# Layer 1 of a four-layer convolution and scan network: other piece boundaries, another order of directions, the last image in chunks

## The chip, the cores and the metric

The kernel runs on one core of a Trainium2 chip. The core has TensorE (PE), VectorE (DVE), ScalarE (ACT), GpSimd (POOL) and SyncE (SP, which here only issues transfers). Each engine works through its own list of instructions in order; an instruction that waits for another engine holds up all that stand behind it. The metric is the time of one execution on the device in microseconds, the median of three runs.

## The reference, cut to what matters

Four layers follow one another on 8 images of 64 channels and 64 x 64 pixels. Only layer 1 is changed. Its reference is this (weights and reshapes left out):

```python
xn = ln(x, 1e-6);  xm, z = split(xn @ in_proj)
xm = silu(conv3x3_depthwise(xm) + conv_b)            # u, 128 channels
xs = [rows, columns, rows reversed, columns reversed]  # 4 directions of u
dts, B, C = split(xs @ x_proj);  delta = softplus(dts @ dt_w + dt_b)
h = exp(delta * A) * h + delta * B * u ;  y = sum_n h * C    # scan over 4096 pixels, 16 states n
y = sum over the 4 directions of y  +  u * sum(D)
y = ln(y, 1e-5) * silu(z);  x1 = x + y @ out_proj
h = conv3x3_depthwise(conv1x1(ln(x1, 1e-6)))
out = x1 + conv1x1(gelu(h1) * h2)
```

Three normalisations over channels (of x, of y, of x1), one depthwise convolution of u and one of the hidden layer belong to each image beside the four scans.

## The kernel before, in words

**The scan stream.** `stream` (L383) works through steps. A step is one image, one direction k and one chunk j of 1024 pixels, and has 16 slots, one for each state n. There are 8 x 4 x 4 = 128 steps and 2048 slots in layer 1. A slot i issues: on POOL the product `hb` = du*B for slot i+2 (L434); on DVE the scan of slot i (L450); the product of the scan with C (L464), on DVE for eleven of the sixteen states and on POOL for states 1, 4, 7, 10 and 13 ("shared"); on PE four matmul instructions that add the product of slot i-2 to the accumulator `acc` (`gather`, L276); on ACT the exponential `dA` of slot i+2 (L441) and the copy of the last column, `carry` (L1148). `dA` has 2 buffers, `hb` and `hc` have 3, `acc` has 1. At the end of a step `drain` (L1157) adds `acc` to the image's y: for direction k = 0 it is a copy on ACT (L1163), for the other three an addition on DVE (L1165); for the two column directions, k = 1 and 3, the view of y is strided.

**The work between the slots.** Everything else of an image is written as a generator that yields between pieces. `Task` (L217) wraps one; `advance` (L367) issues one piece of the first task in the queue `behind` in each slot. A piece that ends with `yield True` holds the only PSUM buffer for such work (`pp`, one buffer of 128 x 1024, tile `mm`); after `yield` it is free; after `yield False` the next piece does not need it. Three tasks belong to an image: `begin` (L905: normalisation, convolution, u and z), `finish` (L966: normalisation of y, product with z, projection, statistics of the next normalisation) and `feed` (L1015: the hidden layer). When the last step of image b is done, `done` (L1167) appends finish(b), begin(b+2) and feed(b), so that they run in the slots of image b+1.

**Pieces of the hidden layer.** `group` (L1041) issues a convolution as two halves (L842) and a right side (L850), one piece each; then the reader comes in the next piece: Gelu on ACT (L1054), a product on DVE (L1057), Gelu on ACT (L1065). The readers of the other convolution and of the projection are ACT's L951 and L1002.

**The next step's inputs.** `Step.prepare` (L1113) is a task as well: x_proj on PE, the copy `dbl` on ACT (L1120), dt_w on PE (L1128), softplus on ACT (L365), `du` on POOL (L1135). It begins at slot `start` = 1 of the step before. At that slot the loop first runs `while self.held or self.urgent: self.advance(behind)`: all pieces up to the one that gives the PSUM buffer back are issued at once. While prepare holds the buffer, no piece that needs it is issued.

**The end.** After the last slot, what is left in `behind` is issued without any slots: finish and feed of the last image.

Of the kernel before, what the change touches and what calls it, by code (L numbers as in the profile page):

```python
# [16 lines left out]
NB = 8  # L17
# [218 lines left out]
            self.step()  # L236


class Net:
    def __init__(self, ctx, tc, d):  # L240
        self.tc, self.nc, self.d = tc, tc.nc, d
# [138 lines left out]
                return  # L380
            queue.popleft()

    def stream(self, pools, ahead, steps, behind):  # L383

# [139 lines left out]
            decay(i + 2)  # L524
        steps[-1].drain(acc.pop(len(steps) - 1))
        steps[-1].done()
        while behind or self.urgent:
            self.advance(behind)

# [256 lines left out]
    def layer1(self, src, dst):  # L786
        nc, tc, d = self.nc, self.tc, self.d
        mid = self.hbm["x1a"]
        with ExitStack() as ctx:
# [2 lines left out]
            pp = pool("pp", 1, space=PSUM)  # L792
            bp = pool("b", 4), pool("cc", 5)
            pools = (bp, pool("hb", 3), pool("hc", 3), pool("h", 3), pool("pe", 2, space=PSUM), pool("pa", 1, space=PSUM))
            hp, h1 = pool("h3", 3, space=DRAM), pool("h1", 4, space=DRAM)
            hz = pool("hz", 1, space=DRAM).tile([NB, 128, L], F32, name="hz")
            centd, cent1 = self.load(cp, "centd"), self.load(cp, "cent1")
# [55 lines left out]

            def place(rows, normed, g, b):

                for r in range(2):
                    yield False
                    at = slice(r * C, r * C + C)
                    nc.scalar.activation(
                        rows[at, :, 1 + r : 1 + r + HW],  # L860
                        normed[at].rearrange("p (a b) -> p a b", b=HW),
                        AF.Identity,
                        bias=b[at],
                        scale=g[at],
                    )

            def statistics(hold, centred, halves, eps):

                rs = p1.tile([128, 32], F32, name="rs")
                for c in range(4):
                    ps = yield from centred(c)
                    sq = tp.tile([128, T], F32, name="tmp")
                    nc.scalar.activation(sq, ps, AF.Square)
                    yield
                    ps = pp.tile([128, T], F32, name="mm")
                    if halves:
                        for r in range(2):  # L880
                            at, o = slice(r * C, r * C + C), slice(r * 512, r * 512 + 512)
                            nc.tensor.matmul(ps[:1, o], mean[at, 0:1], sq[at, o], start=True, stop=True)
                    else:
                        self.mm(ps[:1], mean[:, 1:2], sq)
                    yield True
                    ms = tp.tile([1, T], F32, name="tmp")
                    nc.scalar.copy(ms, ps[:1])
                    nc.scalar.dma_start(rs[c * 32 : c * 32 + 32, :], ms.rearrange("o (p e) -> o p e", e=32))
                    yield
                yield False  # L890
                nc.scalar.activation(rs, rs, AF.Sqrt, bias=eps)
                yield False
                nc.vector.reciprocal(rs, rs)
                yield False
                hold["rs"] = h1.tile([1, L], F32, name="rs")
                nc.sync.dma_start(hold["rs"].rearrange("o (p e) -> (o p) e", e=32), rs)
                yield False
                yield False

# [5 lines left out]
            def begin(b):  # L905
# [37 lines left out]
                for c in range(4):  # L943
                    yield
                    ps = pp.tile([128, T], F32, name="mm")
                    for half in range(2):
                        conv_half(ps, taps, slice(0, 128), pad, c * 16, half)
                        yield True
                    conv_right(ps, taps, slice(0, 128), pad, c * 16)
                    yield True  # L950
                    nc.scalar.activation(hold["u"][:, c * T : c * T + T], ps, AF.Silu, bias=cb)  # L951
                for c in range(4):
                    yield
# [9 lines left out]
                    nc.scalar.activation(z, ps, AF.Silu)  # L963
                    nc.scalar.dma_start(hz[b, :, c * T : c * T + T], z)

            def finish(b):  # L966

                q, rows = b // 2, slice((b % 2) * C, (b % 2) * C + C)
                hold = images[b]
                y = hold.pop("y")  # L970

                def centred(c):
                    ps = pp.tile([128, T], F32, name="mm")
                    self.mm(ps, cent1, y[:, c * T : c * T + T])
                    yield True
                    return ps

                yield from statistics(hold, centred, False, self.eps5)

                def output(c):  # L980
                    at = slice(c * T, c * T + T)
                    inv = spread(hold, c)
                    z = tp.tile([128, T], F32, name="tmp")
                    nc.sync.dma_start(z, hz[b, :, at])
                    x = tokens(src, b, c)
                    yield False
                    yield
                    nc.gpsimd.tensor_tensor(inv, inv, z, ALU.mult)
                    ps = pp.tile([128, T], F32, name="mm")
                    self.mm(ps, cent1, y[:, at])  # L990
                    yield True
                    yield True
                    nc.vector.tensor_tensor(inv, ps, inv, ALU.mult)
                    yield
                    ps = pp.tile([128, T], F32, name="mm")
                    self.mm(ps, w_bias, z, start=True, stop=False)
                    yield True
                    self.mm(ps, w_out, inv, start=False, stop=False)
                    self.sides(ps, self.ident2, x, start=False)
                    yield True  # L1000
                    x = tp.tile([128, T], F32, name="tmp")
                    nc.scalar.copy(x, ps)  # L1002
                    nc.scalar.dma_start(mid[q, rows, at], x[:C])
                    yield
                    ps = pp.tile([128, T], F32, name="mm")
                    for r in range(2):
                        side, o = slice(r * C, r * C + C), slice(r * 512, r * 512 + 512)
                        nc.tensor.matmul(ps[:, o], centd[side], x[side, o], start=True, stop=True)
                    yield True
                    return ps  # L1010

                hold["again"] = {}
                yield from statistics(hold["again"], output, True, self.eps6)

            def feed(b):  # L1015

                q, rows = b // 2, slice((b % 2) * C, (b % 2) * C + C)
                ahead = {}
# [22 lines left out]
                def group(c, cols):  # L1041
                    ps = pp.tile([128, T], F32, name="mm")
                    o = ps[: cols.stop - cols.start]
                    for half in range(2):
                        conv_half(o, hidden, cols, strips[c % 2], 0, half)
                        yield True
                    conv_right(o, hidden, cols, strips[c % 2], 0)
                    yield True
                    return ps

                def gated(c):
# [8 lines left out]
                    ps = yield from group(c, slice(256, 362))  # L1060

                    h = tp.tile([106, T], F32, name="tmp")
                    if c < 2:
                        fetch(c + 2)
                    nc.scalar.activation(h, ps[:106], AF.Gelu)  # L1065
                    yield True
# [11 lines left out]
                    nc.scalar.dma_start(dst[q, rows, c * T : c * T + T], o)  # L1078
                    yield

                fetch(0)
                fetch(1)
                yield False
# [12 lines left out]

            behind = deque()
            begun = {}

            class Step:  # L1100
                start, early, late = 1, 8, True
                shared = (1, 4, 7, 10, 13)
                shaped = staticmethod(lambda t: t)

# [8 lines left out]
                def prepare(self):  # L1113
# [7 lines left out]
                    self.bc = hp.tile([NS, 2, T], F32, name="bc")  # L1121
                    for m in range(2):
                        nc.scalar.dma_start(self.bc[:, m, :], dbl[4 + m * NS : 4 + m * NS + NS])
                    yield
                    pt = pp.tile([128, T], F32, name="mm")
                    for r in range(2):
                        at, o = slice(r * C, r * C + 4), slice(r * 512, r * 512 + 512)
                        nc.tensor.matmul(pt[:, o], dtw[at, k, :], dbl[at, o], start=True, stop=True)  # L1128
                    yield True
                    yield True  # L1130
                    dt = self.dt = p2.tile([128, T], F32, name="dt")
                    net.softplus_act(dt, pt, dtb[:, k : k + 1])
                    yield False
# [22 lines left out]

                def drain(self, acc):  # L1157
                    hold = images[self.b]
                    if self.k == 0 and self.j == 0:
                        hold["y"] = img.tile([128, L], F32, name="img")  # L1160
                    y = view(hold["y"], self.k, self.c)
                    if self.k == 0:
                        nc.scalar.copy(y, like(acc, y))  # L1163
                    else:
                        nc.vector.tensor_tensor(y, like(acc, y), y, ALU.add)  # L1165

                def done(self):  # L1167
                    b = self.b
                    if self.k == 3 and self.j == 3:
# [7 lines left out]
            with tc.manual_schedule():  # L1177
                Task(begin(0)).run()
                if NB > 1:
                    begun[1] = Task(begin(1))  # L1180
                    behind.append(begun[1])
                steps = [Step(b, k, j) for b in range(NB) for k in range(4) for j in range(4)]
                self.stream(pools, (5, 2, 3), steps, behind)


    def layer2(self, src, dst):
# [742 lines left out]
```

## Time and profile before

| what | value |
|---|---|
| median of 3 runs (lowest, highest) | 25963.23 us (25957.64, 25969.22) |
| the profiled execution | 25946.79 us |
| its span | 25944.9 us |
| first scan of layer 1 | 1338.72 us from the span's start |
| last addition of the stream (L1165) | 8808.84 us |
| first matmul of layer 2 (L1229) | 9081.63 us |
| DVE busy in the whole span | 22293.5 us (86%) |
| POOL busy | 21525.5 us (83%) |
| PE busy | 21876.6 us (84%) |
| ACT busy | 14863.5 us (57%) |

The rows of the profile name an engine, a line of the kernel, an operation, its output and inputs by tile names, the busy time and the idle time of the engine just before, with what ended that idle time. A line can be a helper's: L276 is any full-width matmul. A table by windows gives the busy time of each engine in a stretch of the span. DVE and POOL durations overlap a little from one instruction to the next, so sums of durations lie slightly above the time taken.

### The profile page before, as it was taken

The numbers are of one execution on the slowest core, as the hardware profiler recorded it, in microseconds if no ns is written. First come the engines' busy times: TensorE is split into PE (matmuls) and PEld (weight loads), VectorE is DVE, ScalarE is ACT, GpSimd is POOL, SyncE is SP. The second block draws the span as 40 slices with busy tenths as digits, with TensorE's granted clock in tenths as the row PEclk, the third lists the DMA queues.
The fourth block names the chain that finished last, engine by engine and source line by source line (L and its number), as shares of the span: only waits on it lengthen the run. The fifth ranks groups of instructions, "written<-read, shape, count | busy, mean of one in ns | idle before, by whom it ended". The sixth has DMA issues, their size and how long they took to land. (4 is left out here: it accounts for less than half of the span.)

```text
span 25944.9 us, 197961 instructions
## 1 busy us (share of the span) xinstructions
PE 21876.6 (84%) x55754; PEld 8468.4 (33%) x55754; DVE 22293.5 (86%) x12878; ACT 14863.5 (57%) x18690; POOL 21525.5 (83%) x10141
## 2 busy tenths in 40 slices
PE   8777888888888778888888888888878888888888
PEld 5522333333333223322233333333333333333333
DVE  4389889889889579933799999999989999999999
ACT  4355555555555355522566666666666666666666
POOL 0089888889888559930799999999989999999999
PEclk9888999999999899988899999999999999999999
DMA  2289888888888558840455555555544555555554
GB/s 59 78 309 322 296 313 307 297 308 308 298 304 307 189 210 324 324 104 17 130 169 169 170 170 169 169 167 171 168 155 166 170 167 171 170 167 168 169 171 157
DMA packets 1775246, 5292.30 MB, mean 204 GB/s; under 512 B 536624, under 2 KB 542964, under 8 KB 1706304
## 3 DMA queue, kind: packets, MB, share of 16 engines
q1 hardware_dynamic: 1743936, 5207.12, 58.9%
q10 hardware_dynamic: 27136, 63.34, 0.8%
q0 software_dynamic: 3072, 9.18, 0.2%
q8 instruction: 443, 7.26, 0.1%
q14 instruction: 659, 5.40, 0.1%
HBM read 5122.15 MB, written 156.11 MB: 203 GB/s over the span
## 5 line engine op out<-in xcount | busy, mean ns | idle before, releaser
L434 POOL TENSOR_TENSOR hb<-du,bc 128x1024 f32<-128x1024 f32 x4608 | 10755.4, 2360 | 489.9 <-DVE h L450 330.7
L276 PE MATMUL acc<-hc,ident 128*128 128x512 f32 x18816 | 8903.1, 615 | 75.9 <-DVE img L1165 50.9
L441 ACT ACTIVATE dA<-dt,w_A 128x512 f32<-128x512 f32 x8192 | 5662.3, 691 | 4113.5 <-DVE hc L464 3125.0
L450 DVE TENSOR_TENSOR_SCAN dA<-dA,hb 128x1024 f32<-128x1024 f32 x3384 | 7724.8, 2283 | 226.6 <-POOL hb L434 132.9
L276 PE MATMUL acc<-h,ident 128*128 128x512 f32 x7808 | 4584.0, 717 | 2483.9 <-POOL h L464 2483.6
L434 POOL TENSOR_TENSOR hb<-du,b 128x1024 f32<-128x1024 f32 x2048 | 4834.6, 2387 | 736.3 <-DVE h L450 471.5
L276 PEld LDWEIGHTS acc<-hc,ident 128*128 128x128 f32 x18816 | 3685.6, 200 | 5278.5 <-issue 4614.8
L464 DVE TENSOR_TENSOR hc<-dA,bc 128x1024 f32<-128x1024 f32 x3296 | 4034.4, 1224 | 262.1 <-issue 11.1
L441 ACT ACTIVATE dA<-dt,w_l_A 128x1024 f32<-128x1024 f32 x2560 | 2856.1, 1117 | 1126.1 <-DVE hc L464 769.5
L450 DVE TENSOR_TENSOR_SCAN dA<-dA,carry,hb 128x1024 f32<-128x1024 f32 x1320 | 3093.9, 2344 | 205.2 <-ACT dA L441 92.9
L276 PEld LDWEIGHTS acc<-h,ident 128*128 128x128 f32 x7808 | 1557.2, 217 | 5163.9 <-POOL h L464 3334.2
L450 DVE TENSOR_TENSOR_SCAN h<-dA,hb 128x1024 f32<-128x1024 f32 x1352 | 3082.1, 2280 | 80.1 <-ACT carry L1148 43.0
L464 POOL TENSOR_TENSOR h<-h,bc 128x1024 f32<-128x1024 f32 x1312 | 3093.8, 2358 | 14.2 <-DVE h L450 14.2
L464 DVE TENSOR_TENSOR hc<-dA,c 128x1024 f32<-128x1024 f32 x1408 | 1723.4, 1224 | 116.8 <-DMA c<-bc 4.4
L464 POOL TENSOR_TENSOR h<-h,c 128x1024 f32<-128x1024 f32 x640 | 1515.5, 2368 | 30.4 <-ACT carry L1148 30.3
L450 DVE TENSOR_TENSOR_SCAN h<-dA,carry,hb 128x1024 f32<-128x1024 f32 x600 | 1403.5, 2339 | 112.6 <-ACT dA L441 74.0
L441 ACT ACT_TABLE_LOAD x1119 | 1435.7, 1283 | 23.6 <-DVE h L450 3.7
L1148 ACT COPY carry<-dA 128x1 f32<-128x1 f32 x1056 | 166.7, 158 | 1570.9 <-DVE hc L464 1512.3
L1796 PE MATMUL mm<-xn,taps 128*128 128x512 f32 x2048 | 937.8, 600 | 34.1 <-POOL xn L1762 31.9
L659 POOL MEMSET xf<- 128x24 f32 x33 | 4.3, 142 | 909.2 <-PE ps L680 701.7
L1811 PE MATMUL mm<-u,w_xp 128*36 128x512 f32 x1024 | 513.0, 625 | 139.9 <-ACT u L1808 135.0
L1592 POOL COPY strip<-strip 128x66 f32<-128x66 f32 x96 | 23.0, 239 | 729.9 <-DVE strip L1589 697.9
(285 smaller groups left out, 19234.4 us busy)
## 6 DMA issues: line engine op xcount, KB each, us to landing
bc<-bc SPq DMA_DIRECT2D x4096, 512.0 KB
b<-bc SPq DMA_DIRECT2D x2048, 512.0 KB
c<-bc SPq DMA_DIRECT2D x2048, 512.0 KB
bc<-bc SPq DMA_DIRECT2D x512, 1024.0 KB
tmp<-rs SPq DMA_DIRECT2D x96, 512.0 KB
raw<-x SPq DMA_DIRECT2D x64, 512.0 KB
inv<-rs SPq DMA_DIRECT2D x64, 512.0 KB
tmp<-x SPq DMA_DIRECT2D x192, 128.0 KB
```

Of the source, the lines that this page charges most:

```text
L276: self.nc.tensor.matmul(o, lhsT, r, start=start, stop=stop)
L434: nc.gpsimd.tensor_tensor(s.shaped(hb[i]), s.shaped(s.du), B.pop(i), ALU.mult)
L441: nc.scalar.activation(dA[i][:, cut], s.dt[:, cut], AF.Exp, scale=A[:, n : n + 1])
L450: nc.vector.tensor_tensor_scan(h[:, way], dA[i][:, way], hb.pop(i)[:, way], s.first(n), ALU.mult, ALU.add)
L464: engine.tensor_tensor(s.shaped(o), s.shaped(h), CC.pop(i), ALU.mult)
L659: nc.gpsimd.memset(x[:, :, HW:], 0.0)
L1148: nc.scalar.copy(self.carry[:, n : n + 1], h[:, last : last + 1])
L1592: nc.gpsimd.tensor_copy(last[:, 17, :], s[:, 1, :])
L1796: nc.tensor.matmul(tokens(px[:, j * W : j * W + W]), taps[k][:, m, j * 128 : j * 128 + 128], xn[:, :, f : f + HW], start=m == 0, stop=m == 1,)
L1811: nc.tensor.matmul(pd, xp[:, k, j, :], u[:, j * W : j * W + W], start=j == 0, stop=j == 1)
```

## The change

- **A slot more between a convolution or projection and its reader.** `group`, the convolution in `begin` and the projection in `output` end with two `yield True` instead of one.
- **Merged pieces.** In `statistics` the square on ACT and the matmul of the mean over it are one piece, and the copy of the mean no longer ends with a yield of its own. In `prepare` the copy `dbl` and the matmul with dt_w are one piece, and softplus waits for a calm slot (one where neither it nor the next is shared). `start` is 2 instead of 1.
- **`place`.** Before, two ACT instructions wrote the normalised rows into the two halves of the padded tile, in two pieces. Now ACT writes the first half and POOL copies it to the second, in one piece.
- **Order of the directions.** 1, 3, 2, 0 instead of 0, 1, 2, 3. The copy on ACT falls to direction 1; in direction 0, now last, chunk j is row block j.
- **The last image in chunks.** In the last direction of the last image each step appends finish and feed of its own chunk. What is left when the stream ends is issued by `rest`: one piece of the first feed whose finish is over, one piece of the first finish that is not over, and so on. Feeds take their PSUM and SBUF buffers there from the pools of `dA` (2 buffers) and `h` (3 buffers), through `Choice`.

```diff
+class Choice:
+    def tile(self, shape, dtype, name):
+        return self.other.tile(shape, dtype, name=self.name) if self.second else self.pool.tile(shape, dtype, name=name)
...
         steps[-1].done()
+        while self.held:
+            self.advance(behind)
+        if rest is not None:
+            rest()
         while behind or self.urgent:
...
+            pp, tp = Choice(pp, pools[4], "dA"), Choice(tp, pools[3], "h")
...
             def place(rows, normed, g, b):
-                for r in range(2):
-                    yield False
-                    at = slice(r * C, r * C + C)
-                    nc.scalar.activation(
-                        rows[at, :, 1 + r : 1 + r + HW],
-                        normed[at].rearrange("p (a b) -> p a b", b=HW),
-                        AF.Identity,
-                        bias=b[at],
-                        scale=g[at],
-                    )
+                yield False
+                o = rows[:C, :, 1 : 1 + HW]
+                nc.scalar.activation(o, like(normed[:C], o), AF.Identity, bias=b[:C], scale=g[:C])
+                nc.gpsimd.tensor_copy(rows[C:, :, 2 : 2 + HW], o)
...
-            def statistics(hold, centred, halves, eps):
+            def statistics(hold, centred, halves, eps, chunks=range(4)):
...
-                for c in range(4):
+                for c in chunks:
                     ps = yield from centred(c)
                     sq = tp.tile([128, T], F32, name="tmp")
                     nc.scalar.activation(sq, ps, AF.Square)
-                    yield
                     ps = pp.tile([128, T], F32, name="mm")
...
                     nc.scalar.dma_start(rs[c * 32 : c * 32 + 32, :], ms.rearrange("o (p e) -> o p e", e=32))
-                    yield
                 yield False
-                nc.scalar.activation(rs, rs, AF.Sqrt, bias=eps)
+                yield False
+                rs = rs[chunks[0] * 32 : chunks[-1] * 32 + 32]
+                nc.scalar.activation(rs, rs, AF.Sqrt, bias=eps[: len(chunks) * 32])
...
                     conv_right(ps, taps, slice(0, 128), pad, c * 16)
                     yield True
+                    yield True
                     nc.scalar.activation(hold["u"][:, c * T : c * T + T], ps, AF.Silu, bias=cb)
...
                     self.sides(ps, self.ident2, x, start=False)
                     yield True
+                    yield True
                     x = tp.tile([128, T], F32, name="tmp")
                     nc.scalar.copy(x, ps)
...
                     conv_right(o, hidden, cols, strips[c % 2], 0)
                     yield True
+                    yield True
                     return ps
...
+                if part is not None:
+                    fetch(part)
+                    yield False
+                    yield
+                    yield from normed(part)
+                    for c in range(max(0, part - 1), 4 if part == 3 else part):
+                        yield from gated(c)
+                    return
...
+            ends = []
+            def rest():
+                behind.clear()
+                while not all(f.over for _, f in ends):
+                    for n, f in ends:
+                        if n.over and not f.over:
+                            pp.second = tp.second = True
+                            f.step()
+                            pp.second = tp.second = False
+                            break
+                    for n, _ in ends:
+                        if not n.over:
+                            n.step()
+                            break
+            ways = (1, 3, 2, 0)
             class Step:
-                start, early, late = 1, 8, True
+                start, early, late = 2, 8, True
...
                         nc.scalar.dma_start(self.bc[:, m, :], dbl[4 + m * NS : 4 + m * NS + NS])
-                    yield
                     pt = pp.tile([128, T], F32, name="mm")
...
                     yield True
-                    yield True
+                    yield CALM
                     dt = self.dt = p2.tile([128, T], F32, name="dt")
...
-                    if self.k == 0:
+                    if self.k == ways[0]:
                         nc.scalar.copy(y, like(acc, y))
...
+                    if self.k != ways[3]:
+                        return
+                    if b == NB - 1:
+                        ends.append([Task(finish(b, range(self.c, self.c + 1))), Task(feed(b, self.c))])
+                        behind.extend(ends[-1])
+                    elif self.j == 3:
...
-                steps = [Step(b, k, j) for b in range(NB) for k in range(4) for j in range(4)]
-                self.stream(pools, (5, 2, 3), steps, behind)
+                steps = [Step(b, k, j) for b in range(NB) for k in ways for j in range(4)]
+                self.stream(pools, (5, 2, 3), steps, behind, rest)
```

More of the change, by code (lines that the diff above doesn't have):

```diff
@@ L236, in run, with __init__ @@
             self.step()
+class Choice:
+    def __init__(self, pool, other, name):
+        self.pool, self.other, self.name, self.second = pool, other, name, False
+    def tile(self, shape, dtype, name):
+        return self.other.tile(shape, dtype, name=self.name) if self.second else self.pool.tile(shape, dtype, name=name)
 class Net:
@@ L381, in advance, with stream @@
             queue.popleft()
-    def stream(self, pools, ahead, steps, behind):
+    def stream(self, pools, ahead, steps, behind, rest=None):
         nc = self.nc
@@ L894, in statistics @@
                 yield False
-                hold["rs"] = h1.tile([1, L], F32, name="rs")
-                nc.sync.dma_start(hold["rs"].rearrange("o (p e) -> (o p) e", e=32), rs)
+                if chunks[0] == 0:
+                    hold["rs"] = h1.tile([1, L], F32, name="rs")
+                row = hold["rs"][:, chunks[0] * T : chunks[-1] * T + T]
+                nc.sync.dma_start(row.rearrange("o (p e) -> (o p) e", e=32), rs)
                 yield False
@@ L964, in begin, with finish @@
                     nc.scalar.dma_start(hz[b, :, c * T : c * T + T], z)
-            def finish(b):
+            def finish(b, chunks=range(4)):
                 q, rows = b // 2, slice((b % 2) * C, (b % 2) * C + C)
                 hold = images[b]
-                y = hold.pop("y")
+                y = hold["y"]
+                sums, again = hold.setdefault("sums", {}), hold.setdefault("again", {})
                 def centred(c):
@@ L976, in centred @@
                     return ps
-                yield from statistics(hold, centred, False, self.eps5)
+                yield from statistics(sums, centred, False, self.eps5, chunks)
                 def output(c):
                     at = slice(c * T, c * T + T)
-                    inv = spread(hold, c)
+                    inv = spread(sums, c)
                     z = tp.tile([128, T], F32, name="tmp")
@@ L1010, in output, with feed @@
                     return ps
-                hold["again"] = {}
-                yield from statistics(hold["again"], output, True, self.eps6)
-            def feed(b):
+                yield from statistics(again, output, True, self.eps6, chunks)
+            def feed(b, part=None):
                 q, rows = b // 2, slice((b % 2) * C, (b % 2) * C + C)
@@ L1062, in gated @@
                     h = tp.tile([106, T], F32, name="tmp")
-                    if c < 2:
+                    if c < 2 and part is None:
                         fetch(c + 2)
@@ L1158, in drain @@
                     hold = images[self.b]
-                    if self.k == 0 and self.j == 0:
+                    if self.k == ways[0] and self.j == 0:
                         hold["y"] = img.tile([128, L], F32, name="img")
                     y = view(hold["y"], self.k, self.c)
-                    if self.k == 0:
+                    if self.k == ways[0]:
                         nc.scalar.copy(y, like(acc, y))
@@ L1168, in done @@
                     b = self.b
-                    if self.k == 3 and self.j == 3:
+                    if self.k != ways[3]:
[4 more added lines that the diff above has]
+                    elif self.j == 3:
                         behind.append(Task(finish(b)))
```

## The prediction

> **What bounds the kernel now.** I first read the page's table of 40 slices (only slices 3 to 14 are layer 1's), then busy time by windows, one per image of layer 1, then what DVE waited for there, and last the timeline of single stalls and of the end.
>
> ```profile
> core 0: us, PE busy (x) PEld busy (x) DVE busy (x) ACT busy (x) POOL busy (x), PEclk, DMA share, GB/s
> ...
> 3135.00:4084.00 949.00, 805.89 (x1821) 301.50 (x1821) 842.61 (x469) 504.19 (x627) 838.63 (x367) 0.93 0.87 305
> ...
> 8811.00:9082.00 271.00, 192.62 (x481) 64.61 (x482) 20.46 (x19) 46.79 (x50) 11.93 (x9) 0.89 0.17 48
> ```
>
> An image costs 949 us; DVE and POOL are each busy 840 us of them, so neither is clearly the bound, and some 107 us per image are stalls of both. The end, 271 us, has DVE and POOL idle. Undisturbed slots, just before the end, take 53.07 us for 16 (from the addition L1165 at 8709.10 to that at 8762.19): 3.32 us each.
>
> ```profile
> engine line waited for: us in total, times, longest us
> DVE tmp L1057 <- PE mm L850: 243.7, 28, 13.5
> DVE dA L450 <- ACT carry L1148: 115.5, 83, 3.9
> DVE dA L450 <- ACT dA L441: 89.1, 60, 6.0
> DVE h L450 <- ACT carry L1148: 74.4, 27, 5.0
> DVE h L450 <- ACT dA L441: 36.1, 20, 2.4
> DVE tmp L993 <- POOL tmp L988: 24.2, 20, 2.7
> DVE tmp L1068 <- ACT tmp L1065: 16.6, 8, 4.2
> ```
>
> These are DVE's waits from 2300 to 8811 us. They come to about 640 us, 95 per image in images 1 to 6: some 35 in L1057, 48 behind ACT (carry and dA), 12 others. ACT is itself held by PE:
>
> ```profile
> ACT u L951 <- PE mm L850: 100.6, 24, 5.9
> ACT tmp L1002 <- PE mm L320: 98.9, 21, 7.8
> ACT tmp L1054 <- PE mm L850: 80.3, 28, 5.3
> ACT tmp L1065 <- PE mm L850: 62.9, 20, 4.9
> ```
>
> One stall, DVE's rows and then PE's:
>
> ```profile
> 3887.60 1.23 DVE L464 TENSOR_TENSOR hc<-dA,c 128x1024 f32<-128x1024 f32 x1
> 3894.41 1.23 DVE L1057 TENSOR_TENSOR tmp<-mm,tmp 128x1024 f32<-128x1024 f32 x1 [5.59 <-PE mm L850]
> ...
> 3889.71 1.88 PE L276 MATMUL acc<-hc,ident 128*128 128x512 f32 x4
> 3891.52 2.85 PE L850 MATMUL mm<-strip,hright 64*128 64x512 f32 x12
> ```
>
> PE was busy without a gap from 3876 on; the reader was issued too early. In the image shown by the first table, L1057 waited 11.42, 5.59, 9.87 and 6.84 us. The two long ones stand at slot 1 of a step, where the hold on PSUM is flushed and two convolution pieces and their reader are issued together.
>
> **What the Trainium skill says.** "Perfetto Trace Analysis", section Optimization Strategy, says to look for gaps on the most contended engine and for what ends them; the waits above are that list. "ScalarE: Activation LUTs", What ACT_TABLE_LOAD costs, gives 1283 ns for a load, which the trace shows exactly; the further drain of 1380 ns it adds is not visible here (a load at 3880.51, its dA at 3881.81). "GPSIMD Engine Reference", section 3.1, has two-input work about twice as slow as on DVE; here 2.36 against 1.22 us.
>
> **The change part by part.**
>
> *A slot more.* It is issued behind no further PE work: the gather of that slot comes after the convolution in PE's list. So a wait shrinks by one slot, 3.4 us: 5.59 becomes 2.2, 6.84 becomes 3.4. Pieces per image, counted from the yields: begin 67 to 60, finish 74 to 64, feed 90 to 98; 231 becomes 222, so all still fits in an image's 256 slots. Laying them out slot by slot with `start` 2, one L1057 per image still falls into a flush (about 12 us, as 9.9 to 13.5 now), three do not (2.2 + 2.2 + 3.4); but two of the Gelu L1065 now are flushed together with their reader L1068, which then waits for the convolution and 1.02 us of Gelu: about 7.3 each. Feed's waits: 12 + 8 + 15 + 5 for the rest = 40, against 45 now. The begin convolution: waits behind ACT of 15 in that image, to 5, since the spacing of L951 grows by a slot that also covers its flush. The projection L1002: 19 to 12; one of four is flushed. Statistics, z and others: 16 to 14. Sum 95 to 71: 24 per image, 6 images 144. Image 7 (69 now, finish and feed alone) gets chunks of its own: 4. Image 0 (31 now, one begin): 10. Together **-158**.
>
> *Merged pieces.* PE waits for ACT's Square (1.01 us) or dbl (1.01 us) inside the piece, the gather queued behind. PE already waits like this after dbl (63.5 + 63.3 + 61.9 us in three rows) and DVE waited for a gather 0.9 us in all, so three hc buffers hide it: 0. Without that cover: 96 squares + 128 dbl, about 1.5 us each beyond the slack, +336. A gain beyond what the fewer pieces bring I exclude: nothing idles for them. CALM puts softplus at slot 5; its two table loads, 2.57 us, delay dA at an unshared slot; 0.
>
> *Order of directions.* DVE's drain takes 2.33 us strided and 1.21 us flat. Before, directions 1 and 3 are strided and 2 flat; after, 3 strided, 2 and 0 flat. 4 x 1.12 x 8 = **-36**. The copy on ACT turns strided: 1.01 us to perhaps 2 (DVE's ratio; no row shows it), hidden in ACT's 445 idle us per image, uncovered +32.
>
> *place.* ACT loses 1.24 us, POOL gains a copy of 64x1024. Nearest row: L1256, 64x512 in 612 ns, so 1.2 us, 9.8 per image. POOL's 107 idle us hide most while DVE does its own 1.22 us product in the same stretch; I charge 2 per image: **+16**. Bounds 0 and 78.
>
> *The end.* Now, from the last addition to layer 2: statistics, 4 outputs of 14 us, then 4 gated chunks of 37 to 41, as these show:
>
> ```profile
> 8808.84 2.32 DVE L1165 TENSOR_TENSOR img<-acc,img 128x1024 f32<-128x1024 f32 x1 [2.08 <-PE acc L276]
> ...
> 8911.05 0.35 DVE L893 RECIPROCAL rs<-rs 128x32 f32<-128x32 f32 x1 [12.40 <-ACT rs L891]
> ...
> 8943.34 1.23 DVE L1057 TENSOR_TENSOR tmp<-mm,tmp 128x1024 f32<-128x1024 f32 x1 [19.93 <-PE mm L850]
> ...
> 8984.43 1.22 DVE L1057 TENSOR_TENSOR tmp<-mm,tmp 128x1024 f32<-128x1024 f32 x1 [19.37 <-PE mm L850]
> ```
>
> 272.8 us from 8808.84 to 9081.63. After: chunk 0 is done 46 slots before the stream ends. finish(0) and feed(0) take some 32 pieces, steps' prepare blocks three slots of sixteen, so about half of finish(1) is done too; left are half of finish(1), finish(2) and (3), feed(1), (2), (3). A finish of one chunk, from rows of the end: centre, square, mean, copy 6, store and root 4, store, reload and hz 8.5, POOL product 2.3, then 10.3 to the second mean and 2.5: 34 to 37. A gated chunk with two PSUM buffers is bound by PE: three convolutions of 8.25 and 6.4 of projection = 31.2. Half a finish 13; finish(2) beside feed(1), and finish(3) beside feed(2), each at most 37 against 50 alone (7 fetch, 5 norm, 31.2, 6 chain): 54 with some holding up; feed(3) 7 + 5 + 62.4 + 4 = 80. 13 + 54 + 54 + 80 = 201: **-70**. Bounds: 165 (everything overlaps except feed(3) and one finish with its fetches) and 250.
>
> Sum against the profiled execution: 25946.8 - 158 - 36 + 16 - 70 = 25699. The median lies 16.4 above that execution, so **25715**. Differences of 0.2% (52 us) are about what can be told from no change.
>
> **The rivals.**
> - *Stalls go almost altogether* (all ACT and DVE waits on PE fall under a slot, flushes too): some 30 per image left, which is 65 x 6 + 50 in place of 158: about 25430. For it: non-flushed waits are near one slot. Against: flushes stay.
> - *PE's backlog returns.* A gated chunk holds 31 us of convolution and twenty slots' gathers of 1.75, 66, beside x_proj; DVE's twenty slots are 66. PE is the bound there, so what L1057 no longer waits comes back as waits for gathers and L1068. The loop gains only the drains less POOL's copies, the end its 70: 25873.
> - *Slower: the merged pieces.* If hc's three buffers do not hide PE's wait for ACT, 336 is added and outweighs 248: 26050. It decides above 1.1 us lost at each of 224 places. Against it: the 0.9 us above.
> - *The change doesn't do what it says:* feeds and finishes in turn serialise, 37 + 50 each time; the end is then 267 and gains nothing: 25780, inside the likeliest one's range.
>
> **How the numbers follow.** As worked out, serialising included: 0.60, own range 25600 to 25830. Stalls gone: 0.12. Backlog: 0.20. Slower: 0.08. Faster by over 0.2% needs less than 25911: nearly all of the first two and most of the third, 0.86; same 0.07; slower 0.07. Half of the second rival lies below 25500 and all of the slower above 25895, with a sliver of the backlog: range 25500 to 25895.
>
> **What would show it.** DVE's wait at L1057: about 20 per image instead of 35, with L1068 rising to 15; ACT's at L951, L1002, L1054 each under half; images of 920 us; L1165 at 1.2 us in two of three directions; POOL's copy at 1.2 us; about 200 us from the last addition to L1229. Wrong if DVE waits for gathers (hc) or hb for more than 10 us per image, or if the end stays above 250.

## The result, and the profile after

| | before | after |
|---|---|---|
| median | 25960.43 us (25927.02 to 25969.22) | 25709.2 us (25706.78 to 25713.52) |
| ratio, 95% interval | | 0.9906 (0.9889 to 0.9923) |
| profiled execution, its span | 25946.79, 25944.9 us | 25708.36, 25706.6 us |

The predicted time was 25715 us. The span is 238.3 us shorter. The timelines of both kernels tell where; image b runs from the first scan of its slot 0 to that of the next image.

| stretch | before | after | difference | predicted |
|---|---|---|---|---|
| up to the first scan | 1338.7 | 1336.2 | -2.5 | 0 |
| image 0 | 861.4 | 886.5 | **+25.1** | -12.5 |
| images 1 to 6 | 5691.0 | 5548.8 | -142.2 | -159 |
| image 7, to the last addition | 917.7 | 908.6 | -9.1 | -6.5 |
| last addition to layer 2's first matmul | 272.8 | 177.5 | -95.3 | -70 |
| layers 2 and 3 | | | -14.3 | 0 |

The predicted column is the sum's terms laid on the stretches: 24 for the slot, 4.5 for the drains and 2 for POOL's copy per image, and so on. The last row is not the change's: no instruction of those layers was touched, and in the fourteen kernels of this document they take between 16834 and 16864 us.

Image 2 and the end, by windows of the kernel after:

```profile
core 0: us, PE busy (x) PEld busy (x) DVE busy (x) ACT busy (x) POOL busy (x), PEclk, DMA share, GB/s
3149.50:4074.00 924.50, 789.41 (x1808) 297.16 (x1808) 834.91 (x468) 498.86 (x619) 848.54 (x373) 0.94 0.89 313
8677.00:8858.00 181.00, 162.45 (x443) 56.14 (x443) 21.11 (x21) 39.54 (x45) 11.73 (x10) 0.97 0.18 52
```

The images 1 to 6 took 948.5 us in the mean and now take 924.8. From the first scan of image 2 to that of image 3, DVE's busy time fell from 839.9 to 835.1 us, which is the flat additions (24.2 to 19.2). POOL's rose from 835.7 to 848.7: eight copies of 1.04 us make 8 of these 13, the rest is not accounted for. At the end PE is busy for 162 of 181 us, where it was 193 of 271.

DVE's waits in the loop of the kernel after (what it waited for, us in total, times, longest):

```profile
DVE dA L460 <- ACT carry L1190: 160.0, 116, 3.9
DVE tmp L1084 <- ACT tmp L1081: 69.7, 13, 5.4
DVE tmp L1007 <- POOL tmp L1002: 66.6, 27, 4.3
DVE tmp L1073 <- PE mm L866: 56.1, 26, 6.6
DVE h L460 <- ACT dA L451: 51.3, 25, 4.4
DVE dA L460 <- ACT dA L451: 50.6, 43, 1.8
```

L1073 is L1057 of before: 243.7 us became 56.1. L1084 is L1068: 16.6 became 69.7, in 13 waits that are all alike. ACT's waits for PE fell with it: for the convolution of u from 100.6 us to 0.8, for the projection (L1017, was L1002) from 98.9 to 41.5, for the two Gelus from 80.3 and 62.9 to 10.9 and 23.4. DVE's waits for `carry` and `dA` at the scan together fell less, from 315.1 (four rows of before) to 264.9 us (160.0 + 51.3 + 50.6, and 3.0 in a row not shown). Another row rose: at the product L1007 (L993 before) DVE waited 35.2 us, 24.2 of them for POOL, and now 67.0, 66.6 of them for POOL. That is 5 us per image, which the prediction did not have; why POOL's product comes later there is open. In the mean of images 1 to 6, DVE's stalls went from 94.9 to 75.6 us: 19 us, and 4.5 more came from the drains.

The hidden layer in image 2, from DVE's timeline of the kernel after:

```profile
3719.59 1.23 DVE L1073 TENSOR_TENSOR tmp<-mm,tmp 128x1024 f32<-128x1024 f32 x1 [0.49 <-PE mm L866]
3739.06 1.23 DVE L1084 TENSOR_TENSOR tmp<-mm,tmp 42x1024 f32<-42x1024 f32 x1 [5.29 <-ACT tmp L1081]
3801.02 1.23 DVE L1073 TENSOR_TENSOR tmp<-mm,tmp 128x1024 f32<-128x1024 f32 x1 [6.21 <-PE mm L866]
...
3917.12 1.23 DVE L1084 TENSOR_TENSOR tmp<-mm,tmp 42x1024 f32<-42x1024 f32 x1 [5.42 <-ACT tmp L1081]
```

A flush is here what the loop issues at once at slot `start` of a step, up to the release of PSUM. What is not flushed waits at most 1.1 us in images 1 to 6. What is flushed at slot 2 of a step waits 5.3 to 6.2 (6.6 once): three of these per image.

Image 0 has one stall that the kernel before had not. First DVE's row, then what PE and ACT did meanwhile, for one of the four chunks of begin's statistics, and at last the next `carry`:

```profile
1381.36 0.35 DVE L903 RECIPROCAL rs<-rs 128x32 f32<-128x32 f32 x1 [29.10 <-ACT carry L1190]
```

```profile
1359.07 1.13 PE L330 MATMUL mm<-tmp,w_centd 64*128 64x512 f32 x4 [1.10 <-ACT tmp L896]
1360.28 1.02 ACT L886 ACTIVATE tmp<-mm 128x1024 f32<-128x1024 f32 x1 [1.25 <-PE mm L330]
1361.35 1.02 PE L891 MATMUL mm<-tmp,mean 64*1 64x512 f32 x4 [1.15 <-ACT tmp L886]
1362.42 1.00 ACT L896 COPY tmp<-mm 1x1024 f32<-1x1024 f32 x1 [1.12 <-PE mm L891]
...
1374.64 0.16 ACT L1190 COPY carry<-dA 128x1 f32<-128x1 f32 x1 [0.61 <-ACT tmp L896]
```

And the end, on DVE and then PE (the matmul is layer 2's first):

```profile
8680.08 1.23 DVE L1207 TENSOR_TENSOR img<-acc,img 128x1024 f32<-128x1024 f32 x1 [2.08 <-PE acc L286]
...
8695.63 0.34 DVE L903 RECIPROCAL rs<-rs 32x32 f32<-32x32 f32 x1 [12.54 <-ACT rs L901]
...
8739.07 0.34 DVE L903 RECIPROCAL rs<-rs 32x32 f32<-32x32 f32 x1 [0.40 <-ACT rs L901]
...
8785.50 0.35 DVE L903 RECIPROCAL rs<-rs 32x32 f32<-32x32 f32 x1 [14.66 <-ACT rs L901]
...
8857.62 1.55 PE L1277 MATMUL ps<-x,w_cent 128*128 128x512 f32 x3 [1.13 <-ACT h L1093]
```

The three reciprocals of 32 rows are the second statistics of chunks 1, 2 and 3: the phases of the end last 15.5, 43.4, 46.4 and 72.1 us.

### The profile page after: what moved, and what is told of

Its sections match the earlier page's. It is cut to its first block, busy times and chain, and to the rows that moved or that the text cites. A ratio compares the mean times of both kernels' runs of the same rounds, so it can differ in the third digit from the quotient of the medians.

```text
span 25706.6 us, 198113 instructions
## 1 busy us (share of the span) xinstructions
PE 21763.6 (85%) x55754; PEld 8441.0 (33%) x55754; DVE 22248.8 (87%) x12884; ACT 14830.2 (58%) x18642; POOL 21624.2 (84%) x10205
```

## The experiments

All are edits of the changed kernel, but one. Each was timed beside the kernel before, and kernels are compared by their ratios to it; 0.001 is 26 us. The changed kernel has 0.9906.

| kernel | median us | ratio (95% interval) | against the change, us |
|---|---|---|---|
| three slots of before | 25785.58 | 0.9934 (0.9920, 0.9949) | +73 |
| prepare of before | 25765.39 | 0.9928 (0.9913, 0.9942) | +57 |
| both column directions added (order 2, 1, 3, 0) | 25747.65 | 0.9918 (0.9902, 0.9935) | +31 |
| last image whole | 25794.66 | 0.9940 (0.9925, 0.9955) | +88 |
| place on ACT alone | 25698.84 | 0.9905 (0.9888, 0.9921) | -3 |
| begin's statistics apart | 25607.84 | 0.9865 (0.9850, 0.9880) | -106 |
| Square in a piece of its own | 25715.30 | 0.9910 (0.9896, 0.9925) | +10 |
| a release after each chunk | 25677.90 | 0.9900 (0.9885, 0.9914) | -16 |
| feed nine slots later | 25626.85 | 0.9877 (0.9863, 0.9892) | -75 |
| begin of image 1 five slots later | 25676.80 | 0.9898 (0.9883, 0.9913) | -21 |
| both moves | 25590.49 | 0.9867 (0.9851, 0.9884) | -101 |
| before, with the three slots alone | 25968.48 | 1.0011 (1.0002, 1.0020) | +272 |

The intervals are +-40 us wide, mostly from the runs of before. Where a difference is small, the reading rests on the trace.

### The parts undone

**The three extra slots**

```diff
                     conv_right(ps, taps, slice(0, 128), pad, c * 16)
                     yield True
-                    yield True
...
                     self.sides(ps, self.ident2, x, start=False)
                     yield True
-                    yield True
...
                     conv_right(o, hidden, cols, strips[c % 2], 0)
                     yield True
-                    yield True
```

> The changed kernel without the three extra slots between a convolution or projection and its reader; all else stays. Prediction's theory (the reader was issued too early): VectorE's wait in the product after the second convolution rises from 8 us per image to 20 or more, ACT's waits for convolution and projection double, images 1 to 6 go from 925 us to 945, the whole kernel is 110 to 150 us slower than the changed one, about 25840. Rival (fewer and merged pieces and the later start of prepare brought the gain): less than 30 us slower, about 25730.

Images 1 to 6 took 933 to 937 us, 10 more than with the slots, image 7 some 17 more. DVE waited 28 us per image at the product after the second convolution (L1070 here; 127.6 us that the profile puts down to PE and 64.0 for which it names no engine), and not 8; in return hardly any product waited for a flushed Gelu (8.9 us in all, and not 69.7). So the reader was indeed issued too early, but the slots earn 73 us net and not 110 to 150: taking them away also moves the flushes.

**The order of the directions**

```diff
-            ways = (1, 3, 2, 0)
+            ways = (2, 1, 3, 0)
```

> The changed kernel with the directions in the order 2, 1, 3, 0: VectorE has two strided additions per image again, ACT's copy is flat; the last direction stays 0, so the chunks at the end stay. Prediction's theory: 32 additions of 2.33 instead of 1.21 us, 36 us slower. Rival (GpSimd is as full as VectorE and hides it): less than 12 us slower.

As expected, and the strided copy on ACT shows no cost. Images 1 to 6 are 5.5 us longer each, 4 x 1.12 for the drains and 1 more. The rows of the additions in layer 1's loop say the same of before and after: 84 of them took 169.5 us, and then 135.5.

**The last image in chunks**

```diff
-                    if b == NB - 1:
+                    if False:
...
-                self.stream(pools, (5, 2, 3), steps, behind, rest)
+                self.stream(pools, (5, 2, 3), steps, behind)
```

> The last image is finished and fed whole, behind the loop, as in the kernel before; all else is as in the changed kernel. My theory: the end, from the last addition to layer 2's first matmul, goes from 177.5 us back to about 273, and image 7 gets a little shorter (it no longer carries chunk 0's work), by 5: about 25800 us. Rival (the turns cost image 7 what they save behind it): image 7 shorter by 40 or more and the time within 30 us of the changed kernel's 25709.

The end took 259.5 us (8653.12 to 8912.6) and not 177.5, and image 7 was 7.3 us shorter. So the chunks save 82 and cost 7 in the loop. 13 of the 95 us that the end gained are not theirs: the whole end is that much shorter than before's 272.8.

**The copy on POOL**

```diff
                 yield False
-                o = rows[:C, :, 1 : 1 + HW]
-                nc.scalar.activation(o, like(normed[:C], o), AF.Identity, bias=b[:C], scale=g[:C])
-                nc.gpsimd.tensor_copy(rows[C:, :, 2 : 2 + HW], o)
+                for r in range(2):
+                    at = slice(r * C, r * C + C)
+                    o = rows[at, :, 1 + r : 1 + r + HW]
+                    nc.scalar.activation(o, like(normed[at], o), AF.Identity, bias=b[at], scale=g[at])
```

> The right half of the placed rows is written by a second ACT instruction, as in the kernel before, in the same piece, so no slot moves; POOL's copy of 1.04 us is gone, eight times an image. The prediction charged the copy 2 us per image, 16 in all: then about 25693 us. Rival (POOL has the room, ACT has not): ACT's 1.24 us goes back onto dA and carry, for which DVE waits 40 us per image, and the time rises by 10 to 40 us. If both are hidden: 25709 within 8.

Images 1 to 6 took 926.1 us in the mean, with the copy 924.8. Neither POOL's 1.04 us nor ACT's 1.23 us shows: both are hidden, and the 16 us charged were not there.

**The piece boundaries and start of prepare**

```diff
-                start, early, late = 2, 8, True
+                start, early, late = 1, 8, True
...
+                    yield
                     pt = pp.tile([128, T], F32, name="mm")
...
-                    yield CALM
+                    yield True
```

> The changed kernel with prepare as before: start at slot 1, the matmul with dt_w a piece of its own, softplus not tied to a calm slot. Prediction's theory: this part costs and gains nothing (0 within 30 us), apart from other places at which the flush falls. Rival: keeping other work from between dbl and dt_w was a gain of its own: 60 us slower or more. Second rival, from the trace after: VectorE waits 1.25 us at slot 5 of nearly every step, with exponentials behind dbl; the old order takes these away and is 30 to 100 us faster.

Images 1 to 6 took 932 to 935 us, 8 more, and image 7 took 19 more; image 0 took 866.5 us, 20 less, as the flush of 29 us is gone. In all the kernel is 57 us slower, so this part is not worth 0. But with `start` at 1 every flush moved to slot 1, where the three of image 3 wait 9.9, 5.9 and 5.9 us (6.2, 5.3 and 5.4 in the changed kernel). The part of the trace that no flush reaches is image 0 from slot 96 on, ten steps in which `behind` is empty. They took 523.7 us before, 518.8 here and **527.4** in the changed kernel. In these slots three additions turned from strided to flat (3.4), and the waits for POOL are 1.3 shorter: 523.7 less 4.7 is 519.0, so this kernel has just those gains, and the changed prepare costs 8.6 us in ten steps, 0.86 each. This is where (ACT's and DVE's timelines at slot 5 of a step, first in the changed kernel, then in this one):

```profile
1712.59 1.12 ACT L451 ACTIVATE dA<-dt,w_l_A 128x1024 f32<-128x1024 f32 x1 [2.10 <-DVE h L460]
1713.65 0.17 ACT L1190 COPY carry<-h 128x1 f32<-128x1 f32 x1
...
1713.82 2.36 DVE L460 TENSOR_TENSOR_SCAN dA<-dA,carry,hb 128x1024 f32<-128x1024 f32 x1 [1.25 <-ACT carry L1190]
```

```profile
1700.95 1.12 ACT L451 ACTIVATE dA<-dt,w_l_A 128x1024 f32<-128x1024 f32 x1
1702.90 2.33 DVE L460 TENSOR_TENSOR_SCAN dA<-dA,carry,hb 128x1024 f32<-128x1024 f32 x1
1703.02 0.19 ACT L1191 COPY carry<-h 128x1 f32<-128x1 f32 x1 [0.95 <-DVE h L460]
```

The exponential is the one issued in slot 3, and DVE's scan of slot 5 reads the `dA` that it writes. In the changed kernel it starts only when the scan of slot 4 has ended, and DVE waits 1.25 us for it. (The row names the `carry` copy, which ended as the scan began, at 1713.82; but the exponential ended at 1713.71, and it is the scan's own input.) In the kernel with the old prepare the same exponential starts before the scan of slot 4 ends; the wait for that scan stands one instruction later, at the copy that reads it, and DVE does not wait. In the changed kernel nearly every step that copies `carry` has this stall; the last step of a direction, which copies none, has it in the first direction of an image alone. At slot 5 DVE stalls for 132 us in all eight images of the changed kernel, 18 before and 15 here. The calm slot does not do it: in undisturbed steps softplus stands at the same place of ACT's list in all three kernels, behind the exponential that slot 4 issues. What moved is x_proj and `dbl`, one slot later (`start` and the merged piece); these two weren't told apart, nor what this part gains elsewhere to be worth 57 us in spite of the stall.

### What the merged pieces cost

**The begin's statistics in separate pieces again**

```diff
                     nc.scalar.activation(sq, ps, AF.Square)
+                    if apart:
+                        yield
...
                     nc.scalar.dma_start(rs[c * 32 : c * 32 + 32, :], ms.rearrange("o (p e) -> o p e", e=32))
+                    if apart:
+                        yield
```

`apart` is set for begin's statistics alone.

> The changed kernel with the pieces of the statistics in begin kept apart again (square; mean; copy), finish's left merged. Theory from the trace after: merged pieces give the PSUM buffer back only after all four chunks, so in image 0 the flush at slot 2 issues them all at once and VectorE waits 29 us; apart, image 0 is 25 us shorter (861 instead of 886) and the other images stay within 4 us, because there the statistics do not meet a flush; in all about 25 us faster than the changed kernel. Rival (image 0 is longer for the order of directions or the later prepare): image 0 stays at 886 us and the kernel at 25709.

The gain was four times what was expected: image 0 took 869.7 us, and images 1 to 6 took 908 to 916, where the changed kernel's take 922 to 929. My first reading was that merging itself costs: PE waits for Square inside the piece. But a piece more also moves all that follows. Counted from the yields, the feed now starts eleven slots later, and its flushes at slot 2 of a step catch other pieces: one product L1084 with its Gelu and not two, and an L1073 whose convolution had been issued before. The kernels that follow tell these apart.

**The wait inside the piece alone**

```diff
                     nc.scalar.activation(sq, ps, AF.Square)
+                    if apart:
+                        yield True
```

PSUM stays held, so nothing behind moves.

> The begin's statistics have their own slot between Square and mean again, but keep PSUM held across it, so the flushes in the feed and all that follows stay where they are in the changed kernel; only PE's wait for Square inside the piece is gone. If that wait is what the merged pieces cost: images 1 to 6 shorter by 5 to 12 us each, 25635 to 25680 us. If the place of the flushes and the hold made the gain: 25709 within 15 us, image 0's flush of 29 us at slot 2 the same or longer.

Nothing was gained: images 1 to 6 took 922.6 to 925.0 us, and image 0's stall is still 29.05 us. PE's wait for Square inside a merged piece of begin costs nothing that can be seen.

**The place of the flushes alone**

```diff
                 fetch(0)
                 fetch(1)
                 yield False
-                yield
+                for _ in range(10):
+                    yield
```

> Nine empty slots ahead of the feed, which move it so that each image has one flush at L1084 (with its Gelu) instead of two, and nothing else changes; statistics pieces stay merged. Taking the begin's statistics pieces apart gained 101 us, and it moved the feed in the same way (11 slots). If the place of the flushes made that gain: images 1 to 6 shorter by 10 to 14 us each as there, image 0 unchanged, about 25635 us. If the merged pieces themselves cost it (PE waiting for ACT inside them): only the one L1084 wait of 5.3 us less per image, about 25677 us; if nothing hangs on the place, 25709 within 12.

Images 1 to 6 took 912.1 to 916.6 us, 10.5 less, and image 0 stayed at 885.8. In image 3 all eight products of the hidden layer stand in the same slots as with the pieces apart. DVE's stalls per image fell from 75.6 to 65.3 us, 10.0 of it just ahead of the scan of slot 2, where a flush is issued. Of DVE's waits in the loop of this kernel:

```profile
DVE tmp L1073 <- PE mm L866: 41.3, 26, 3.1
DVE tmp L1084 <- ACT tmp L1081: 37.1, 7, 5.3
```

Seven waits at L1084 and not 13, and the longest at L1073 is 3.1 us and not 6.6: as counted. Nine empty slots bring 63 of the 77 us that images 1 to 6 gained with the pieces apart; the other 14 are not accounted for.

**Half of the separation**

```diff
                     nc.scalar.dma_start(rs[c * 32 : c * 32 + 32, :], ms.rearrange("o (p e) -> o p e", e=32))
+                    if apart:
+                        yield
```

> Half of taking the begin's statistics apart: a slot after each chunk of them, which releases PSUM, while Square and mean stay in one piece. Four slots more per image, so the feed moves by four, not by eleven. By the count each image's flushes then hold one L1084 with its Gelu and two L1073 (two L1084 and one L1073 in the changed kernel, one and one where the pieces are all apart). If only the places of the flushes matter: images 1 to 6 within 4 us of the changed kernel's 925, and image 0 shorter by 17 to 25, about 25690 us. If the release itself makes the gain: images 1 to 6 shorter by 8 to 14 each as with all pieces apart, about 25620 us.

Images 1 to 6 took 922.7 us in the mean, 2 less than the changed kernel's, and image 0 took 870.5, 16 less (17 to 25 were expected). Per image the waits at L1084 halved (10.7 to 5.4) and those at L1073 rose (8.3 to about 12), as the count had it. The release after each chunk is not what gains in images 1 to 6; where the flushes then fall is.

**Image 0**

```diff
                 ahead = {0: tokens(src, b, 0)}
-                yield False
+                for _ in range(6 if b == 1 else 1):
+                    yield False
```

> begin of image 1 starts five slots later, so that no flush finds its merged statistics under way; images 1 to 7 are issued slot by slot as in the changed kernel. My theory: the wait of 29 us at L903 in image 0 is the whole of its 25 us loss, image 0 takes about 862 us instead of 886.5, images 1 to 7 are as they were: about 25684 us. Rival (image 0 is longer for another reason, the new start of prepare or the copies on POOL): image 0 above 880 and the time within 8 of 25709.

Image 0 in this kernel, and then in the changed one, by windows from its first scan to that of image 1:

```profile
1326.43:2187.99 861.56, 649.40 (x1317) 245.26 (x1318) 812.91 (x449) 435.40 (x554) 833.79 (x363) 0.89 0.92 323
```

```profile
1336.18:2222.70 886.52, 655.22 (x1317) 247.31 (x1318) 813.41 (x449) 436.43 (x554) 833.71 (x363) 0.87 0.89 314
```

The same work, the same numbers of instructions, 24.9 us apart, as expected; images 1 to 7 are as they were. A chunk of merged statistics ends and the next begins without giving PSUM back, so the flush at slot 2 goes on through all four chunks: PE, ACT and PE again, one after the other, with the next scans' `carry` and `dA` behind them on ACT, as the rows of image 0 above show.

**Both moves**

The two edits above in one kernel.

> Both moves at once: begin of image 1 five slots later, and nine empty slots ahead of each feed; no instruction is added or taken away. If a flush costs by what it holds and where it falls, and nothing else, the two gains add: image 0 about 859 us, images 1 to 6 about 914 each, and 25709 less 82 less 32 makes about 25595 us. If they share a cause (PE's clock, or work pushed into another image), less than the larger of the two is added: 25620 us or more.

They add: image 0 took 859.7 us, images 1 to 6 took 906.6 to 913.1. At 0.9867 this equals the kernel with the begin's statistics apart, and both beat the change by 0.4% without adding or removing an instruction.

### What the merged pieces are for

**Before, with the three slots alone** (the three added lines of the first diff, in the kernel before)

> The kernel before with the three extra slots alone. Counted from the yields, an image then needs more pieces than it has slots: the begins of images 4 to 7 are unfinished when their image is due and 16 to 38 pieces of each are issued at one slot, and at the end a feed more than before is left over. My theory: PE's work for them, some 60 to 90 us each, shows as stalls at the ends of images 3 to 6, and the end grows from 273 to about 450 us, against 24 us gained per image: slower, about 26100 us. Rival: the three slots carry the gain without the merged pieces: about 25800 us.

No faster than before (ratio 1.0011), though not as slow as I expected. Images 1 and 2 took 896.9 and 910.1 us, 53 and 36 less than before, and then the overflow came: 937.3, 969.6, 969.3, 962.6. One stall at the end of image 4 in this kernel:

```profile
5860.14 2.36 DVE L450 TENSOR_TENSOR_SCAN dA<-dA,carry,hb 128x1024 f32<-128x1024 f32 x1 [46.68 <-ACT dA L441]
```

There the due begin of image 5 is issued at one go (38 pieces, by the count). The end grew from 272.8 to 351.2 us, not to 450. So the slots need room, and the merged pieces make it: the extra slots add 20 to the 231 pieces of an image, and what is merged in statistics and in `place` takes 29 away; 256 slots have to hold them beside the prepares.

## Why the prediction was right, and where its steps were not

The time was met within 6 us, and the likeliest case was the one that came: the readers wait less, the drains are flat, the end overlaps. That the sum fits so closely is in part luck. Image 0 came out 38 us and images 1 to 6 came out 17 us worse than forecast, the end 25 us better, and layers 2 and 3, which the change does not touch, ran 14 us shorter.

- **A slot more, -158.** Images 1 to 6 came near: stalls from 95.2 to 72.1 us in image 3, where 71 was worked out. The composition was not met. L1057 and L1068 together were put at 35 us per image; they measured 19, since what is not flushed waits at most 1.1 us (not 2.2 to 3.4), and a flush 5.3 to 6.6 (not 7.3 and 12). The rest, 36 in the sum, measured 53: 13 us of it is the stall at slot 5 in the next step of this list, and 5 us are the wait for POOL at L1007. Nor is the gain the slots' alone: taken out, they cost 73 us, and without the merged pieces they gain nothing.
- **CALM and the start of prepare, 0.** This step failed. It named softplus' table loads at slot 5; softplus stands there before the change too. What the runs show is an exponential that starts 1.25 us too late for the scan of slot 5: 0.86 us per undisturbed step, 13 us in image 3. The part as a whole, undone, costs 57 us, so other effects of it, the place of the flush among them, outweigh the stall. Neither size was in the sum.
- **Merged pieces, 0.** Right for what it argued, as far as it was tested: with a slot of its own for begin's Square nothing changes (0.9910 against 0.9906), and DVE waits for gathers no more than before. The merged `dbl` was not undone alone. The three rows of waits after `dbl` that the argument used, 63.5, 63.3 and 61.9 us, are the weight loads'; PE's matmuls waited 34.4, 31.3 and 33.9 us there. What the argument did not ask is what a piece without a release does under a flush. In image 0 that is 24.9 us. Without it the image takes 861.6 us, as before the change (861.4), so the 12.5 us forecast for it did not come either: DVE's waits for ACT at the scans there went from 21.6 to 28.6 us. The flush rule was in the code and used for the readers, but the statistics were not run through it.
- **Flushes in the feed.** Two L1084 and one L1073 per image were counted rightly. That they could be moved by nine empty slots, for 75 us, was not seen; it is as large as the end's whole term.
- **Order of directions, -36.** Right: -31 by the ratios (+-40), -34 in 84 additions of the loop. ACT's copy got as slow as supposed (mean 1914 ns, was 1012), and no cost of it shows.
- **`place`, +16.** Nothing measurable; the copy's 1.2 us were 1.04.
- **The end, -70.** The mechanism was right and the size off: 177.5 us, not 201, of which the turns bring 82 and 13 came without them. The phases 13, 54, 54 and 80 measured 15.5, 43.4, 46.4 and 72.1. The 54 was the 50 us of a feed's chunk alone and 4 for holding up; a finish and a feed by turns took less than the 50.

The rivals: stalls remain (72 to 80 us per image, not 30), so they did not go altogether. PE's backlog did not return: PE is busy for 789 of 924.5 us, and DVE waited for a gather's buffer 0.2 us in all. The merged pieces did not cost 336 us: the whole kernel is 251 us faster. The turns did not serialise (177.5 us, not 267).

## What to carry to other kernels

Where pieces of other work are issued between the slots of a loop, what they cost depends on where they fall against the loop's own period. Count that slot by slot for each edit, since an edit that only adds or removes a piece moves every later one; a control that adds empty slots alone tells an edit's own effect from the move. When a rule issues all pieces up to the next release at once, the pieces between two releases are the unit to look at: merging pieces saves slots, and removing the release between them makes that unit longer.

A stretch in which nothing but the loop runs, as image 0 from slot 96 on here, shows a cost of under 1 us per step that is hard to see in the busy images; once it is known, sorting DVE's stalls by slot shows it there too. Where a row of the profile names what ended a wait, look also at what the waiting instruction reads: here the named copy ended last, but the scan needed the exponential before it.

## What the runs showed of the hardware

A strided view slows ACT's copy out of PSUM about as much as DVE's addition. From the rows of the loop, ACT's copy before (flat) and after (strided), then POOL's one-input copy (shapes and count, busy us and mean ns, idle us before):

```profile
L1163 ACT COPY img<-acc 128x1024 f32<-128x1024 f32 x27 | 27.3, 1012 | 23.8 <-ACT dbl L1120 22.7 <-issue 1.0
```

```profile
L1205 ACT COPY img<-acc 128x1024 f32<-128x1024 f32 x27 | 51.7, 1914 | 15.7 <-PE acc L286 7.3 <-ACT tmp L1017 4.3 <-ACT tmp L896 4.1
```

```profile
L875 POOL COPY strip<-strip 64x1024 f32<-64x1024 f32 x32 | 33.1, 1035 | 118.1 <-ACT strip L874 77.2 <-ACT strip L1048 32.5 <-ACT carry L1190 7.4
```

ACT's copy took 1914 ns against 1012, and DVE's addition 2.33 against 1.21 us. The Trainium skill, "SBUF — State Buffer", section Door 1: The DMA port swizzle, says that each access that crosses to a new 16-byte line pays a penalty, and gives no size for it; both engines' numbers here, with an inner step of 64 elements, fit that, at 1.9 times the flat time, though no run here tells it from another cost of the stride. POOL's copy of 64 x 1024 takes 1.04 us, its product of 128 x 1024 takes 2.35.

In the changed kernel ACT waits for the scan of slot 4 at an exponential, and not at the `carry` copy behind it that reads this scan: in the step shown ACT stands idle for 2.10 us ahead of the exponential, until that scan ends, and the copy comes after it. Why the wait stands there is open.
